# Weighting and summing the gathered tile of the first layer on GpSimd instead of VectorE

## The chip, the core and the metric

The kernel runs on one core of one Trainium2 chip. The metric is the device time of one execution in microseconds (us). One core has TensorE (PE in the profile, with its weight loads as PEld), VectorE (DVE), ScalarE (ACT), GpSimd (POOL) and SyncE (SP), which only starts DMA transfers here.

## What is computed

The whole kernel is a four-layer network on four images of 128 channels and 64 x 64 pixels, in fp32. The change is in the first layer alone, a deformable convolution. For each pixel and each of 8 groups of 16 channels, nine taps are read at places that the data itself moves:

```python
val = xf @ w_value + b_value
om = (xf @ w_off + b_off).reshape(N, P, G, OM)      # 18 offsets and 9 masks per group
...
for dy, dx, wgt in ((0, 0, (1 - ty) * (1 - tx)), (0, 1, (1 - ty) * tx), (1, 0, ty * (1 - tx)), (1, 1, ty * tx)):
    iy, ix = (y0i + dy, x0i + dx)
    acc = acc + gather(iy, ix) * (wgt * valid(iy, ix))[..., None]
out = (acc * mask[..., None]).sum(axis=3)
out = out.reshape(N, P, C) @ w_out + b_out
```

After it follow a batch norm and a SiLU. The layers behind it (a state-space convolution, attention maps with a feed-forward net, two mixtures of experts around an attention) are not touched.

## The kernel before

The first layer treats most pixels without a gather. For pixels whose offsets are all at most 1, the sum over the taps is a weighted sum over a 5 x 5 neighbourhood, and the neighbourhood is read as plain rows. The work goes in 32 **rounds**, 8 for each image; a round is a piece of 512 pixels (`r` is its number). In each round, for each of the five rows `k` of the neighbourhood:

- `multiply` is one VectorE instruction, `pr<-v,wt` of 128x2560, which multiplies the row's five shifted copies by their weights. `pr` has two buffers.
- `accumulate` is five TensorE matmuls `acc<-pr,ident` of 128x512, which add the five products up in PSUM.
- between them stand the steps of later rounds: `project` (TensorE, `psp<-wn,xr`), `evict` (VectorE, `omw<-psp,bn` and `vb<-psp,bn`), and on VectorE the interpolation weights of the next round (`tent`, `Q`, `t`, `wt`).

The pixels with an offset over 1 are rare. They are the **exceptions**: at most 128 of an image are collected by one-hot matmuls into one tile of 128 rows, and for this tile alone a 7 x 7 neighbourhood is gathered. The generator `exceptions(n)` does it for image `n`: 49 indirect DMAs that GpSimd issues, seven for each row `s` of the neighbourhood, each of which fetches one row of 128 channels per exception into `px`. `px` has two buffers, and row `s + 1` is issued before row `s` is used. Each row is multiplied by its weights (`total<-px,wt` for the first row, `px<-px,wt` for the other six) and added to `total` (six times `total<-total,px`). At the end seven matmuls `pe<-ident,total` sum the seven columns and turn the tile, and a second matmul applies `w_out`. The result, `tw`, is added to the rounds' outputs by the matmul `pO<-oT,tw` in `finish`. Last, `settle` adds the output `sl` to the image on GpSimd (`X<-X,sl`).

The order is written out by hand. `InOrder` keeps every instruction of an engine in program order, so an instruction that waits holds up all that stand behind it on its engine. The generator is advanced once for each `k` of a round:

```python
if r >= 0 and r % NQS == 1 and r < LAST_R:
    extra = exceptions(r // NQS)
...
if extra is not None:
    next(extra, None)
```

With `NQS = 8` it starts in an image's round 1. It yields twice for each row of the neighbourhood, so its last add stands at the end of the image's round 3, and the matmuls `pe<-ident,total` stand at the first step of round 4, in TensorE's order ahead of all further products of that round. Below, **idx** is the start of an image's first gather (it waits for the indices `idx` that VectorE makes), and **pe1** the start of `pe<-ident,total`. Nearly all instructions of the layer have line L81 in the profile, that of the helper in `InOrder`; so they are told apart by their tiles.

Of the kernel before, what the change touches and what calls it, by code (L numbers as in the profile page):

```python
# [11 lines left out]
ALU = mybir.AluOpType  # L12
# [75 lines left out]
class Kernel:  # L88
# [33 lines left out]
    def layer0(self):  # L122
# [7 lines left out]
        tc, nc, X = self.tc, self.nc, self.X  # L130
# [11 lines left out]
        with ExitStack() as outer:  # L142
            fp = outer.enter_context(tc.tile_pool(name="d0x", bufs=1))
            over = fp.tile([1, 1], I32, name="over")
            with ExitStack() as ctx:
# [142 lines left out]
                nc = InOrder(tc)  # L288
# [11 lines left out]
                def tents(om, m, r):  # L300

                    D = 2 * r + 1
                    o = om[:, 0:18 * m]
                    tent = wp.tile([P, D, 18 * m], F32, name=f"tent{r}", tag="tent")
                    ab = wp.tile([P, 18 * m], F32, name=f"ab{r}", tag="t0")
                    for d in range(-r, r + 1):
                        if abs(d) == r:
                            k = R2 + r - 1
                            nc.scalar.activation(tent[:, d + r, :], o, AF.Relu, bias=shift[:, k:k + 1],
                                                 scale=float(d // r))  # L310
                        else:
                            nc.scalar.activation(ab, o, AF.Abs, bias=shift[:, d + R2:d + R2 + 1])
                            nc.scalar.activation(tent[:, d + r, :], ab, AF.Relu, bias=self.ones[:, 0:1],
                                                 scale=-1.0)
                    return tent
# [135 lines left out]
                def exceptions(n):  # L451
                    oc = wp.tile([P, NO + 1, G], F32, name="oc")
                    ocf = oc.rearrange("p j g -> p (j g)")
                    nc.scalar.copy(ocf, rare[n][:, 0:(NO + 1) * G])
                    idx = wp.tile([P, W2, W2], I32, name="idx")
                    nc.vector.tensor_scalar(idx, reach, oc[:, NO, 0:1], None, ALU.add)
                    flat = tabs[n].rearrange("x y c -> (x y) c")
                    wt = wp.tile([P, W2, W2, G], F32, name="wt2")

                    def gather(s):  # L460
                        px = qp.tile([P, W2, P], F32, name="px")
                        for u in range(W2):
                            nc.gpsimd.indirect_dma_start(
                                out=px[:, u, :], out_offset=None, in_=flat,
                                in_offset=bass.IndirectOffsetOnAxis(ap=idx[:, s, u:u + 1], axis=0))
                            if u == 3:
                                yield
                        return px

                    px = yield from gather(0)  # L470
                    yield "weights"
                    for _ in weights(ocf, tents(ocf, G, R2), wt, G, R2):
                        pass
                    total = wp.tile([P, W2, P], F32, name="total")
                    for s in range(W2):
                        after = (yield from gather(s + 1)) if s + 1 < W2 else None
                        dst = px if s else total
                        nc.vector.tensor_tensor(
                            dst.rearrange("p u (g c) -> p (u g) c", c=CG),
                            px.rearrange("p u (g c) -> p (u g) c", c=CG),  # L480
                            wt[:, s].rearrange("p u g -> p (u g)").unsqueeze(2).to_broadcast([P, W2 * G, CG]),
                            ALU.mult)
                        if s:
                            nc.vector.tensor_tensor(total, total, px, ALU.add)
                        px = after
                        yield
                    ps = pt.tile([P, TG * P], F32, name="pe1", tag="pt")
                    for u in range(W2):
                        nc.tensor.matmul(ps[:, 0:P], total[:, u, :], self.ident, start=(u == 0), stop=(u == W2 - 1))
                    eT = sm.tile([P, P], F32, name="eT", bufs=1)  # L490
                    nc.scalar.copy(eT, ps[:, 0:P])
                    yield
                    ps = pt.tile([P, TG * P], F32, name="pe2", tag="pt")
                    nc.tensor.matmul(ps[:, 0:P], eT, w_out, start=True, stop=True)
                    tw = sm.tile([P, P], F32, name="tw", bufs=2)
                    nc.scalar.copy(tw, ps[:, 0:P])
                    mended[n] = tw
# [88 lines left out]
                for r in range(-4, LAST_R + 1):  # L586
# [5 lines left out]
                    if r >= 0 and r % NQS == 1 and r < LAST_R:  # L592
                        extra = exceptions(r // NQS)
# [79 lines left out]
                nc = plain  # L673
# [1815 lines left out]
```

## Time and profile before

| what | value |
| --- | --- |
| time, median of 3 runs | 5625.36 us (5615.98 to 5626.08) |
| profiled execution, its own time | 5626.52 us |
| its span (first to last instruction) | 5624.8 us |
| busy in the span: PE, DVE, ACT, POOL | 5034.6, 3967.9, 3095.8, 3025.3 us |
| idx to pe1, images 0 to 3 | 148.4 to 258.7, 410.2 to 521.6, 673.1 to 778.7, 927.6 to 1031.8 us |
| last `X<-X,sl` of the first layer | starts at 1141.82 us |

The first layer is thus about a fifth of the span. The profile shows one execution. Its 1.7 us beyond the span lie ahead of the first and behind the last instruction. A line of a group gives the number of instructions, their busy time, the mean of one in ns, and the idle time of the engine ahead of them with what ended it. A line of a table by stretch gives, for each engine, busy us and the number of instructions, then TensorE's granted clock (1.00 is full), the DMA share and GB/s.

### The profile page before, as it was taken

What the parts mean: (1) busy time and instruction counts of PE and PEld (TensorE: products, weight loads), DVE (VectorE), ACT (ScalarE), POOL (GpSimd) and SP (SyncE); (2) the same over time, 40 slices, a digit from 0 to 9 for tenths busy, and PEclk for the clock granted to TensorE, in tenths of its full rate; (3) what the DMA queues carried; (4) which work ended last, traced back from release to release, by engine and by line L of the source; (5) the groups of instructions that cost most, each with busy time, mean ns of one, the idle gap of its engine ahead of it and who ended that gap; (6) DMA issues with size and microseconds to landing.
All of it is one profiled execution on the core that took longest, in us unless ns stands there. A gap on an engine that the chain in (4) does not pass through costs nothing. (4 is left out here: it accounts for less than half of the span.)

```text
span 5624.8 us, 62917 instructions
## 1 busy us (share of the span) xinstructions
PE 5034.6 (90%) x21582; PEld 2263.2 (40%) x21582; DVE 3967.9 (71%) x7776; ACT 3095.8 (55%) x3721; POOL 3025.3 (54%) x2995
## 2 busy tenths in 40 slices
PE   6898988879999859999787999899989998999787
PEld 3454444436656523333443333333333333333343
DVE  6888988758876577886697655566566565665796
ACT  1122222146655445555421788878878887889431
POOL 0525344314444334544498666666666665667597
PEclk8999999989989779999898999999999999999899
DMA  5545454300000110000000000000000000000001
GB/s 173 129 128 127 130 129 121 94 6 3 14 16 16 43 40 1 1 1 1 6 31 30 1 1 1 1 1 1 1 1 1 1 1 1 1 1 1 5 1 60
DMA packets 66746, 185.23 MB, mean 33 GB/s; under 512 B 13158, under 2 KB 16038, under 8 KB 64744
## 3 DMA queue, kind: packets, MB, share of 16 engines
q1 hardware_dynamic: 55792, 163.68, 9.9%
q0 software_dynamic: 6272, 12.86, 1.4%
q10 hardware_dynamic: 4344, 4.50, 0.3%
q8 instruction: 174, 2.85, 0.2%
q14 instruction: 164, 1.34, 0.1%
HBM read 131.63 MB, written 49.36 MB: 32 GB/s over the span
## 5 line engine op out<-in xcount | busy, mean ns | idle before, releaser
L81 POOL TENSOR_TENSOR r<-r 128x512 f32<-128x512 f32 (+1 forms) x1088 | 1349.2, 1240 | 750.8 <-DVE r L81 688.3
L81 DVE TENSOR_TENSOR r<-r,num 128x1024 f32<-128x1024 f32 (+1 forms) x1088 | 964.6, 926 | 626.7 <-PE num L81 555.6
L81 PE MATMUL num<-F,N 32*128 32x512 f32 (+3 forms) x4608 | 1227.1, 614 | 70.2 <-DVE r L81 27.9
L81 PE MATMUL D<-F,G 32*128 32x512 f32 (+3 forms) x4608 | 1247.3, 607 | 33.6 <-ACT r L81 29.9
L81 ACT ACTIVATE r<-r 128x2048 f32<-128x2048 f32 (+4 forms) x610 | 1018.4, 1679 | 50.9 <-POOL r L81 3.8
L81 ACT ACTIVATE r<-D 128x1536 f32<-128x1536 f32 (+1 forms) x544 | 767.3, 1410 | 263.8 <-PE D L81 213.6
L81 PE MATMUL acc<-pr,ident 128*128 128x512 f32 x1600 | 748.3, 618 | 76.2 <-DVE pr L81 76.2
L81 PEld LDWEIGHTS D<-F,G 32*128 32x128 f32 x4608 | 415.6, 187 | 487.8 <-issue 344.9
L81 PE MATMUL acc<-r,v 128*128 128x512 f32 (+3 forms) x1152 | 608.0, 615 | 2.4 <-DVE aT L81 2.4
L1885 PE MATMUL pex<-w_expert_w,vT 128*128 128x512 f32 x1024 | 489.6, 617 | 79.5 <-DVE x L1888 79.4
L81 PEld LDWEIGHTS num<-F,N 32*128 32x128 f32 x4608 | 357.1, 186 | 468.5 <-SPq L81 340.1
L1895 POOL TENSOR_TENSOR x<-x 128x512 f32<-128x512 f32 (+2 forms) x576 | 472.5, 820 | 105.8 <-DVE x L1888 75.8
L81 PEld LDWEIGHTS acc<-pr,ident 128*128 128x128 f32 x1600 | 309.1, 198 | 435.9 <-issue 339.8
L81 DVE TENSOR_TENSOR pr<-v,wt 128x2560 f32<-128x2560 f32 x160 | 452.5, 2833 | 30.1 <-PE acc L81 24.3
L81 PE MATMUL pff<-hid,w_ffn_w2T 128*128 128x512 f32 x1024 | 468.2, 600 | 0.0
L81 POOL DMA_INDIRECT px<-tab,idx x196 | 331.8, 1693 | 227.8 <-DVE idx L81 159.2
L1888 DVE TENSOR_TENSOR x<-pex,gate 128x1024 f32<-128x1024 f32 x256 | 308.8, 1212 | 61.8 <-POOL X L1896 49.9
L81 POOL TENSOR_TENSOR X<-X,sl 128x512 f32<-128x512 f32 x32 | 87.7, 2740 | 491.8 <-ACT sl L81 491.8
L81 PEld LDWEIGHTS acc<-r,v 128*128 128x128 f32 x1152 | 177.1, 191 | 392.5 <-POOL r L81 217.3
L81 ACT ACTIVATE hid<-phh,cols 128x512 f32<-128x512 f32 x320 | 198.9, 685 | 223.9 <-PE phh L81 223.9
L1885 PEld LDWEIGHTS pex<-w_expert_w,vT 128*128 128x128 f32 x1024 | 183.2, 193 | 330.3 <-DVE x L1888 181.6
L81 POOL TENSOR_TENSOR Y<-y,tm 128x64 f32<-128x64 f32 x256 | 115.9, 473 | 323.4 <-DVE w L81 160.7
(562 smaller groups left out, 7139.3 us busy)
## 6 DMA issues: line engine op xcount, KB each, us to landing
v<-tab SPq DMA_DIRECT2D x320, 256.0 KB
oms<-omw SPq DMA_DIRECT2D x32, 432.0 KB
omr<-oms SPq DMA_DIRECT2D x32, 432.0 KB
X<-in_x_dram SPq DMA_DIRECT2D x8, 1024.0 KB
tab<-vb SPq DMA_DIRECT2D x64, 128.0 KB
o<-o SPq DMA_DIRECT2D x32, 256.0 KB
oin<-o SPq DMA_DIRECT2D x32, 256.0 KB
kept<-X SPq DMA_DIRECT2D x4, 2048.0 KB
```

The source lines that it names most:

```text
L81: return lambda *args, **kwargs: self.tc.keep_in_program_order(op(*args, **kwargs))
L1885: nc.tensor.matmul(pex[:, 4 * h:4 * h + 4, :], vT[:, k, :], ew[:, 512 * h:512 * (h + 1)], start=True, stop=True)
L1888: nc.vector.tensor_tensor(x, pex, gate[:, k, :].unsqueeze(2).to_broadcast([P, NE, P]), ALU.mult)
L1895: nc.gpsimd.tensor_tensor(x[:, 0:w, :], x[:, 0:w, :], x[:, w:2 * w, :], ALU.add)
```

## The change

The 13 elementwise instructions of each image's exceptions (seven multiplications by the weights and six additions, all 128x896 in fp32) move from VectorE's program to GpSimd's, at the same places in the program. GpSimd also issues the gathers that fill `px`; it now does so between these instructions. Nothing else in the source changes.

```diff
                     for s in range(W2):
                         after = (yield from gather(s + 1)) if s + 1 < W2 else None
                         dst = px if s else total
-                        nc.vector.tensor_tensor(
+                        nc.gpsimd.tensor_tensor(
                             dst.rearrange("p u (g c) -> p (u g) c", c=CG),
                             px.rearrange("p u (g c) -> p (u g) c", c=CG),
                             wt[:, s].rearrange("p u g -> p (u g)").unsqueeze(2).to_broadcast([P, W2 * G, CG]),
                             ALU.mult)
                         if s:
-                            nc.vector.tensor_tensor(total, total, px, ALU.add)
+                            nc.gpsimd.tensor_tensor(total, total, px, ALU.add)
                         px = after
                         yield
```

In the instruction streams of the changed kernel, GpSimd has for each image 14 gathers, one multiplication, then five times seven gathers, one multiplication and one addition, and last the multiplication and addition of the seventh row. VectorE's stream lacks the 52 instructions, and its other instructions keep their order. The first `pe<-ident,total` of each image waits for GpSimd where it waited for VectorE. On SyncE a few pairs of neighbouring stores (`tab<-vb`, `oms<-omw`) change places.

## Prediction

> **What bounds the kernel now.** I read the page first, then the busy time by stretch, with the cuts at each image's idx and pe1, then the tile px, then the timeline.
>
> The page's costliest groups give the work that shares an engine with the moved instructions:
>
> ```profile
> L81 POOL DMA_INDIRECT px<-tab,idx x196 | 331.8, 1693 | 227.8 <-DVE idx L81 159.2
> ```
>
> By stretch, idx to pe1 and pe1 to the next idx in turn:
>
> ```profile
> core 0: us, PE busy (x) PEld busy (x) DVE busy (x) ACT busy (x) POOL busy (x), PEclk, DMA share, GB/s
> 148.40:258.70 110.30, 88.64 (x226) 43.40 (x226) 99.79 (x147) 20.97 (x52) 81.03 (x49) 0.89 0.54 131
> 258.70:410.20 151.50, 151.26 (x455) 78.74 (x455) 132.33 (x215) 41.43 (x91) 25.38 (x8) 1.00 0.46 127
> 410.20:521.60 111.40, 87.93 (x226) 42.97 (x225) 99.34 (x147) 22.26 (x53) 81.64 (x49) 0.91 0.52 125
> 521.60:673.10 151.50, 151.26 (x455) 78.75 (x455) 132.77 (x216) 41.43 (x91) 25.26 (x8) 1.00 0.47 130
> 673.10:778.70 105.60, 87.72 (x222) 42.34 (x220) 88.28 (x127) 20.79 (x51) 84.75 (x49) 0.90 0.55 129
> 778.70:927.60 148.90, 147.74 (x438) 76.15 (x439) 134.82 (x204) 39.03 (x86) 20.79 (x8) 1.00 0.45 126
> 927.60:1031.80 104.20, 76.96 (x165) 32.72 (x163) 74.86 (x70) 18.56 (x43) 84.42 (x49) 0.87 0.52 114
> 1031.80:1150.00 118.20, 105.28 (x290) 49.45 (x290) 79.55 (x81) 25.30 (x53) 16.26 (x8) 0.97 0.25 67
> ```
>
> From pe1 to the next idx TensorE works without a break (151.26 of 151.50): it is the bound there, nothing lost earlier is made up. From idx to pe1 it idles a fifth of the time, and VectorE is the busiest (99.79 of 110.30 in image 0). But in images 2 and 3 VectorE idles too. The tile px says for what:
>
> ```profile
> L81 POOL DMA_INDIRECT px<-tab,idx x196: 940/1142/3560, 148.4 to 1025.7; - x196
> L81 DVE TENSOR_TENSOR px<-px,wt x24: 1073/1092/1125, 182.1 to 1029.6; 128x896 f32<-128x896 f32 x24
> L81 DVE TENSOR_TENSOR total<-total,px x24: 1091/1091/1093, 183.2 to 1030.7; 128x896 f32<-128x896 f32 x24
> ...
>   DMA px<-tab,idx: 40.5, 19
> ```
>
> GpSimd's gathers fill 95.9, 98.0, 99.4 and 99.0 us (first start to last end) of stretches of 110.3, 111.4, 105.6 and 104.2. So idx to pe1 has two chains of almost one length: VectorE's program, and GpSimd's 49 gathers. A gather takes 0.94 us at best and 1.69 in the mean. The timeline shows where the rest comes from:
>
> ```profile
> 148.07 2.82 DVE L81 TENSOR_TENSOR pr<-v,wt 128x2560 f32<-128x2560 f32 x1
> ...
> 148.45 3.48 POOL L81 DMA_INDIRECT px<-tab,idx  x1 [144.47 <-DVE idx L81]
> ...
> 281.28 2.82 DVE L81 TENSOR_TENSOR pr<-v,wt 128x2560 f32<-128x2560 f32 x1
> ...
> 281.56 3.67 POOL L81 TENSOR_TENSOR X<-X,sl 128x512 f32<-128x512 f32 x1 [5.69 <-ACT sl L81]
> ...
> 284.94 2.98 DVE L81 TENSOR_TENSOR pr<-v,wt 128x2560 f32<-128x2560 f32 x1 [0.83 <-PE acc L81]
> ```
>
> The gather that starts 0.4 us into a product ends 1.0 us after it; the addition that starts 0.3 us into one ends 1.15 us after it, and alone takes 1.26 (at 538.74). GpSimd waits for such a product's end.
>
> **What the Trainium skill says.** "SBUF — State Buffer", section Who interferes with whom: a VectorE instruction with two SBUF inputs contends with a GpSimd instruction that reads SBUF, and whoever came first holds the port pair for the whole instruction. The trace agrees, both ways: beside 3.67 against 1.26 above, one product at 803.00 that met an addition of 1.27 us took 3.93 instead of 2.82. Evictions, which read PSUM, delayed no gather (all of 21 that started in one took 0.94). The same section supposes that descriptor generation does not suffer from a tensor_tensor; here gathers that started in a product took 3.28 us in the median, and the measurement decides. "GPSIMD Engine Reference", section Elementwise — side-by-side cycle accounting, gives 4497 ns for an addition of 2048 columns, 2.2 ns for each. The trace gives 2.1, below.
>
> **The change part by part.** All is per image; the sum is at the end.
>
> *Off VectorE:* 13 x 1.09 = 14.2 us of work, and its waits for px (3.4, 5.0, 14.3 and 27.1 us in the four stretches, the short stops of px among them).
>
> *Onto GpSimd, the instructions themselves.* 896 columns stand in no row, so I take the two nearest families:
>
> ```profile
> L1895 POOL TENSOR_TENSOR x<-x 128x512 f32<-128x512 f32 x192 | 244.7, 1275 | 75.8 <-DVE x L1888 75.8
> ...
> L1895 POOL TENSOR_TENSOR x<-x 128x256 f32<-128x256 f32 x192 | 140.2, 730 | 15.0
> ...
> L81 POOL TENSOR_TENSOR ta<-tri,a 128x1024 f32<-128x1024 f32 x32 | 60.7, 1898 | 0.0
> ...
> L81 POOL TENSOR_TENSOR xw<-tm,wd 128x512 f32<-128x512 f32 x32 | 33.2, 1038 | 1.7 <-ACT tm L81 1.7
> ```
>
> Additions of two full operands: (1275 - 730)/256 = 2.13 ns a column, so 1275 + 384 x 2.13 = 2.09 us. Multiplications by a repeated weight: (1898 - 1038)/512 = 1.68, so 1.04 + 0.65 = 1.69 us. Together 7 x 1.69 + 6 x 2.09 = 24.4 us. From below all cost 1.69 (22.0); from above 2.4 each, with 0.3 us of idle as before every gather (31).
>
> *The gathers:* 49 x (0.94 + 0.30 idle) = 60.9 us without any port wait. Ahead of the last multiplication no further gather hides the landing any more: 2.9 us, as in image 3 today (1026.7 to 1029.6). GpSimd's chain without waits is thus 60.9 + 24.4 + 2.9 = **88.2 us**.
>
> *GpSimd's waits for the port.* Today's gathers average 98.1 us, so they wait 37.2; 2.7 of it behind the 13 instructions that leave VectorE. 34.5 stay. VectorE's other two-input instructions fill 58 to 64 us of a stretch; squares of their durations over twice the stretch give 0.6 us as the mean wait of an arrival at random, gathers have 0.7. I take 0.65 for each multiplication. An addition comes straight behind a multiplication that VectorE may have been waiting out, so VectorE then goes first: I take 1.1. That is 7 x 0.65 + 6 x 1.1 = 11.1 us. In sum 45.6 us of waits in 88.2 + 45.6 = 133.8 us, a share of **0.34**, as long as VectorE runs.
>
> *VectorE's new waits.* An instruction of GpSimd now holds the port for 1.7 to 2.1 us. VectorE wants it some 60% of the time; I take 1.0 us for each of 13, from 0 to 1.9. Its own program then takes, from idx, busy less 14.2, plus its waits for others (7.1, 7.1, 3.0, 2.2 us), plus 13: 105.7, 105.2, 90.1 and 75.9 us (77 in image 3, where TensorE needs as much).
>
> *The wait at pe1.* GpSimd's chain = 88.2 + 0.34 x the time that VectorE runs:
> image 0: 88.2 + 35.9 = 124.1, was 110.3: +13.8
> image 1: 88.2 + 35.8 = 124.0, was 111.4: +12.6
> image 2: 88.2 + 30.6 = 118.8, was 105.6: +13.2
> image 3: 88.2 + 26.2 = 114.4, was 104.2: +10.2
> The sum is **+50 us**. TensorE waits at pe1 some 18 to 37 us, and behind it stand all products of round 4; VectorE fills its two pr buffers and stops. TensorE then starts at half clock: after today's waits ten matmuls took 6.3 to 7.2 us instead of 4.46. I add 2 us an image, 8 in all, from 0 to 14.
>
> *At nothing:* the additions X<-X,sl stand behind pe1 in any case, ScalarE is busy 19% there, the stores that change places on SyncE come in pairs that few us separate, and the later layers move as a whole. The gathers' transfers are the same; they are spread out more.
>
> Against the profiled execution, 5626.5 + 58 = 5684.5; the median of the runs lies 1 us lower: **5684 us**.
>
> **Rivals.** Faster and slower mean by more than 0.2% (11 us), about what a measurement can tell from no change.
>
> *Faster: GpSimd had time to spare.* VectorE sheds 14 us and its waits for px, and would need 93, 92, 77 and 63 us if GpSimd held it up in nothing. For it speaks that VectorE is the busiest engine of the stretch. Against it, that GpSimd's gathers already fill nine tenths of it. The point is where GpSimd's chain falls below 108 us, so where its waits fall under 20 us an image, while the gathers alone wait 34 today. At half of that (17 us) the chain is 105: -3 an image; with none at all, 93, 92, 88 and 88, or -70. I take -35: 5591 us. 8%.
>
> *Slower still: the port alternates.* After each GpSimd instruction VectorE takes the port, and all 13 wait 2.2 us, close to a whole product; VectorE is held 1.9 us each. The share becomes (34.5 + 28.6)/151 = 0.42, VectorE runs 117, 117, 102 and 89 us, the chain is 137, 137, 131 and 126: +27, +26, +25, +22, and 10 for the clock: 5736 us. The back-to-back order of multiplication and addition speaks for it; against it, that many instructions of VectorE between products read PSUM or less than 1 us. 20%.
>
> *No change: made up behind pe1.* VectorE, ahead by two products, would have to speed up TensorE; at 151.26 of 151.50 it can't. 4%, about 5626 us.
>
> **How the numbers follow.** The waits as in the sum: 68%, 5684 us, with its own range 5642 (4 us an image, no clock) to 5735. Slower 0.88, within 0.2% 0.04, faster 0.08. The range 5640 to 5750 leaves out the faster cases, no change, and the far end of the alternation, under 20% together.
>
> **What would show it.** Right: in the table by stretch, idx to pe1 grows by 10 to 15 us while pe1 to the next idx stays at 149 to 151; TensorE waits for GpSimd's total at pe1, 15 us or more; GpSimd's 128x896 take 2 us at best and 2.3 to 3.2 in the mean; VectorE no longer waits for px, and some of its products take 3.5 us or more. Wrong: TensorE reaches pe1 after GpSimd is done, or the stretch shrinks; then the share of waits, 0.34, is the step that failed.

## The result and the profile after

The changed kernel takes 5700.03 us in the median of 6 runs (5683.76 to 5717.25), the kernel before, on the same chip, 5625.72 (5611.88 to 5641.41). The ratio is 1.0129, with a 95% interval of 1.0108 to 1.0149: 74 us slower. The profiled execution has a span of 5698.4 us, 73.6 more than that of before.

All of it is in the first layer. Its last `X<-X,sl` starts at 1213.60 us, where it started at 1141.82: 71.8 us later. What comes after it takes 4484.8 us in this profile, against 4483.0. Over all profiles of this study that rest moves between 4464 and 4492 us, although no kernel changed it. So the experiments below are judged by the start of the last `X<-X,sl`, beside the medians.

By stretch, with the cuts at idx and pe1 of each image as in the prediction:

```profile
core 0: us, PE busy (x) PEld busy (x) DVE busy (x) ACT busy (x) POOL busy (x), PEclk, DMA share, GB/s
147.50:267.40 119.90, 87.13 (x227) 43.09 (x225) 106.65 (x144) 21.14 (x53) 104.76 (x62) 0.88 0.52 124
267.40:421.30 153.90, 153.66 (x453) 80.50 (x454) 131.56 (x206) 41.27 (x90) 22.91 (x8) 0.98 0.45 122
421.30:548.20 126.90, 88.40 (x227) 43.58 (x225) 106.75 (x150) 22.42 (x54) 111.78 (x62) 0.85 0.48 120
548.20:701.70 153.50, 153.26 (x453) 80.38 (x454) 124.71 (x199) 41.27 (x90) 25.34 (x9) 0.99 0.43 120
701.70:826.70 125.00, 84.85 (x221) 41.25 (x219) 104.63 (x133) 20.95 (x52) 109.87 (x62) 0.86 0.50 121
826.70:976.70 150.00, 149.76 (x437) 77.92 (x438) 120.58 (x184) 38.76 (x85) 23.27 (x9) 0.98 0.42 115
976.70:1103.70 127.00, 69.43 (x165) 30.46 (x163) 82.05 (x73) 18.56 (x43) 111.92 (x62) 0.80 0.47 106
```

From idx to pe1 an image now takes 119.9, 126.9, 125.0 and 127.0 us, where it took 110.3, 111.4, 105.6 and 104.2: 67 us more in sum. From pe1 to the next idx it takes 1 to 2.5 us more, at a granted clock of 0.98 to 0.99 in place of 1.00, and TensorE is busy throughout. The tile px, and for its last line the tile total, say what happens in the first kind:

```profile
L81 POOL DMA_INDIRECT px<-tab,idx x196: 940/1034/3791, 147.5 to 1095.0; - x196
L81 POOL TENSOR_TENSOR px<-px,wt x24: 1705/1723/3675, 194.4 to 1099.8; 128x896 f32<-128x896 f32 x24
L81 POOL TENSOR_TENSOR total<-total,px x24: 2067/2084/4677, 196.2 to 1101.6; 128x896 f32<-128x896 f32 x24
L81 POOL TENSOR_TENSOR total<-px,wt x4: 1721/1724/1726, 176.2 to 1006.9; 128x896 f32<-128x896 f32 x4
...
  PE pe L81: 99.0, 4
```

A multiplication takes 1.72 us and an addition 2.08 on GpSimd, and TensorE waits 99 us at pe1, in four waits. In the kernel before this last line was

```profile
  PE pe L81: 2.2, 1
```

GpSimd's instructions do not wait for their gathers to land: in the tile px, the list of what engines sat idle for has `DMA px<-tab,idx` at 40.5 us in the kernel before and not at all in this one. The longest wait at pe1 is in image 3, in the timeline of TensorE:

```profile
1043.47 13.14 PE L81 MATMUL acc<-pr,ident 128*128 128x512 f32 x30 [1.22 <-DVE pr L81]
1103.71 3.36 PE L81 MATMUL pe<-ident,total 128*128 128x128 f32 x14 [47.10 <-POOL total L81]
1106.86 3.47 PE L81 MATMUL acc<-pr,ident 128*128 128x512 f32 x6
```

So TensorE, less its wait, gets to pe1 110.5, 110.1, 99.2 and 79.9 us after idx, 31.7 us earlier in sum than pe1 stood before, and then waits 9.4, 16.8, 25.8 and 47.1 us. VectorE has lost 14.2 us of work an image and its waits for px, and images 0 and 1 get nothing from it. The timeline shows what takes it back, first a product, then additions of one column in the tile `fl`:

```profile
447.69 4.65 DVE L81 TENSOR_TENSOR pr<-v,wt 128x2560 f32<-128x2560 f32 x1 [1.85 <-PE acc L81]
...
447.93 1.73 POOL L81 TENSOR_TENSOR total<-px,wt 128x896 f32<-128x896 f32 x1
...
196.36 2.36 DVE L81 TENSOR_TENSOR fl<-fl 128x1 f32<-128x1 f32 x3
...
196.18 2.08 POOL L81 TENSOR_TENSOR total<-total,px 128x896 f32<-128x896 f32 x1
```

In the kernel before, three such additions were

```profile
170.14 0.55 DVE L81 TENSOR_TENSOR fl<-fl 128x1 f32<-128x1 f32 x3
```

The product takes 4.65 us instead of 2.82, and three tiny additions 2.36 us instead of 0.55, while GpSimd's instruction runs. Taking each VectorE instruction of a stretch over the usual duration of its kind, VectorE is held up 19.0, 13.6, 18.1 and 8.1 us from idx to pe1.

### The profile page after: what moved, and what is told of

It is laid out like the page before. It is cut to its first block, busy times and chain, and to the rows that moved or that the text cites. A ratio compares the mean times of both kernels' runs of the same rounds, so it can differ in the third digit from the quotient of the medians.

```text
span 5698.4 us, 62841 instructions
## 1 busy us (share of the span) xinstructions
PE 5037.1 (88%) x21582; PEld 2270.4 (40%) x21582; DVE 3970.2 (70%) x7724; ACT 3095.5 (54%) x3721; POOL 3129.8 (55%) x3047
## 5 line engine op out<-in xcount | busy, mean ns | idle before, releaser
L81 ACT ACTIVATE r<-r 128x2048 f32<-128x2048 f32 (+4 forms) x610 | 1018.4, 1679 | 50.9 <-POOL r L81 3.9
```

Source lines behind the costliest of these rows:

```text
L81: return lambda *args, **kwargs: self.tc.keep_in_program_order(op(*args, **kwargs))
```

## The experiments

The theory: gathers and sums stand one behind the other on GpSimd, this **chain** is now longer than everything else from idx to pe1, and TensorE waits for its end. The rival: the loss is **VectorE being held at the port** by GpSimd's new instructions.

All numbers below, in one table. "Last X" is the start of the last `X<-X,sl`, less the 1141.8 us of the kernel before; the ratio is to the runs of the kernel before on the same chip. The waits at pe1 and the stretches are sums over the four images.

| kernel | median us | ratio, 95% interval | last X, us | wait at pe1, us | idx to pe1, us |
| --- | --- | --- | --- | --- | --- |
| before | 5625.7 | 1 | 0 | 2.2 | 431.4 |
| changed | 5700.0 | 1.0129 (1.0108 to 1.0149) | +71.8 | 99.0 | 498.7 |
| short_gathers | 5616.5 | 0.9980 (0.9971 to 0.9988) | -6.9 | 0 | 428.3 |
| shed_sums | 5572.8 | 0.9902 (0.9882 to 0.9922) | -50.9 | 0 | 362.2 |
| late_pe1 | 5653.7 | 1.0049 (1.0031 to 1.0068) | +26.7 | 48.1 | a round more |
| six_more_sums | 5746.1 | 1.0206 (1.0183 to 1.0228) | +122.9 | 130.3 | 549.9 |
| three_rows | 5653.6 | 1.0039 (1.0022 to 1.0055) | +25.0 | 2.3 | 456.4 |
| before_late_pe1 | 5641.9 | 1.0012 (1.0003 to 1.0021) | +8.7 | 0 | a round more |
| spread_vector | 5605.5 | 0.9953 (0.9936 to 0.9970) | -26.7 | 4.1 | a round more |

The first four after the changed kernel ran beside runs of the kernel before with a median of 5628.4 us, the last three beside 5633.2.

**short_gathers** cuts the chain and keeps the new instructions.

```diff
-                        for u in range(W2):
+                        nc.gpsimd.memset(px[:, 2:, :], 0.0)
+                        for u in range(2):
...
-                            if u == 3:
+                            if u == 1:
```

> Five of the seven gathers of each row are left out, and GpSimd clears their five columns of px instead (0.6 us), so the sums miss most of the neighbourhood; all 13 products and sums of an image stay on GpSimd as in the changed kernel. Theory of the chain (TensorE waits at pe1 because gathers and sums stand one behind the other on GpSimd): GpSimd's chain falls from 120 to 127 us to about 60, the waits at pe1 (9.4, 16.8, 25.8 and 47.1 us in the changed kernel) are gone, and pe1 comes when VectorE and TensorE get there, about 110, 110, 99 and 80 us after idx: 5590 to 5605 us. Rival (the loss is VectorE being held at the port by the 13 instructions): these are all still there, so 5680 us or more.

TensorE no longer waits at pe1, and the loss is gone: the chain is what made the changed kernel slower. It ends 76 to 78 us after idx here, where 60 were expected, and still 18 us or more ahead of pe1. But the time is only 12 us under that of before, where 23 to 38 were expected. The table by stretch, images 0 to 3:

```profile
148.10:263.90 115.80, 90.57 (x226) 43.86 (x225) 101.47 (x134) 20.98 (x52) 66.06 (x33) 0.88 0.42 109
415.60:530.50 114.90, 90.30 (x226) 43.91 (x225) 102.13 (x134) 22.25 (x53) 66.32 (x33) 0.87 0.42 108
682.20:784.40 102.20, 86.41 (x220) 41.59 (x219) 98.68 (x117) 20.80 (x51) 68.60 (x33) 0.92 0.45 115
931.90:1027.30 95.40, 76.33 (x165) 32.90 (x164) 85.00 (x59) 18.55 (x43) 69.36 (x33) 0.89 0.41 101
```

VectorE is busy 101.5 us in image 0, 1.7 us more than before, with 13 instructions fewer: it is held up 16.4, 17.1, 20.5 and 19.9 us, more than the 14.2 that it shed. So the holds that the rival names are there, though they are not the cause of the loss: they take back what VectorE was relieved of.

**shed_sums** takes the work off VectorE without putting it on GpSimd.

```diff
-                        nc.vector.tensor_tensor(
-                            dst.rearrange("p u (g c) -> p (u g) c", c=CG),
+                        if s == 0:
+                            nc.vector.tensor_tensor(
+                                dst.rearrange("p u (g c) -> p (u g) c", c=CG),
...
-                        if s:
-                            nc.vector.tensor_tensor(total, total, px, ALU.add)
```

> Only the product of the first row stays, on VectorE; the other 12 products and sums of an image are left out on both engines, and all gathers are still issued. It prices what VectorE can gain by shedding them, with nothing put on GpSimd. Theory of the chain: VectorE loses 13.1 us of work and its waits for px (3.4, 5.0, 14.3, 27.1 us), so idx to pe1 takes about 94, 93, 89 and 76 us instead of 110, 111, 106 and 104: near 5546 us (5535 to 5570). Rival (VectorE's load in this stretch does not matter, TensorE is the bound there): above 5600 us. The difference to the run with few gathers is what the port holds cost: about 50 us if VectorE, held 8 to 19 us an image in the changed kernel, gets nothing out of the move.

VectorE's load in this stretch is worth a lot: idx to pe1 falls to 102.5, 101.1, 83.9 and 74.7 us, the time by 55.5. Nothing holds VectorE up here (under 1 us an image). The gain is some 25 us less than expected. One part is that VectorE waits more for TensorE: `rstd` and `bn`, two steps of the batch norm, wait 7.6 us in image 0, where they waited 3.2. And in image 3 the gathers go on for 38 us behind pe1, with the `X<-X,sl` behind them on GpSimd; ScalarE cannot reuse sl:

```profile
ACT sl L81 <- issue: 24.4, 1, 24.4
```

The first of these additions starts at 1003.80 us, right behind the last gather, and TensorE idles 10.3 us in turn; from pe1 to the last X image 3 takes 125.2 us in place of 110.0. Between this run and short_gathers lie 66 us in idx to pe1 and 44 us in the medians. That is mostly the price of the holds, 74 us in sum in short_gathers; the two runs also differ in the engine of the first product and in the gathers.

**late_pe1** leaves everything in place and lets a round of 29 us pass before TensorE asks for the sum; the image's first pieces are finished a round later too.

```diff
+                    for _ in range(5):
+                        yield
                     ps = pt.tile([P, TG * P], F32, name="pe1", tag="pt")
...
-                    aT = qp.tile([P, TG * P], F32, name="aT", bufs=4)
+                    aT = qp.tile([P, TG * P], F32, name="aT", bufs=5)
...
-                    for k, qs in ((4, (0, 1)), (5, (2, 3)), (6, (4,)), (7, (5,)), (8, (6, 7))):
+                    for k, qs in ((5, (0, 1)), (6, (2, 3)), (7, (4, 5)), (8, (6, 7))):
```

> The changed kernel with pe1 and the finishing of the image's first pieces put one round later (five more yields ahead of pe1, one more buffer for aT). All work is done. Theory of the chain: a round of some 29 us now lies over GpSimd's chain. It covers the waits of images 0 to 2 (9.4, 16.8, 25.8 us) all but a few us and 27 of the 47 us of image 3, so about 75 to 80 us come back: 5615 to 5640 us, level with the kernel before. Rival (VectorE held at the port): the holds stay as they are and so does the loss, 5680 us or more.

45 us come back by the last X and 46 in the medians. The rival, which had 5680 us or more, is thus excluded, but 75 to 80 were expected. The waits at pe1 are 0, 0, 14.7 and 33.4 us; the estimate had about 0, 0, a few and 20. Its table by stretch shows the reason, images 2 and 3:

```profile
681.10:817.10 136.00, 108.60 (x295) 53.61 (x293) 128.01 (x169) 26.82 (x66) 120.89 (x62) 0.93 0.58 139
941.30:1080.10 138.80, 92.56 (x220) 40.61 (x218) 104.33 (x88) 23.63 (x54) 123.69 (x62) 0.87 0.50 116
```

GpSimd's chain itself has become longer, 136.0 and 138.8 us instead of 125.0 and 127.0. Its gathers wait 47.2 and 43.6 us beyond their 0.94 us each, where they waited 34.0 and 36.2. In the changed kernel VectorE stands still while TensorE waits at pe1, and issues 15 products from idx to pe1 in each image; here it goes on, and issues 20 in images 2 and 3. The wait at pe1 partly pays for itself.

**before_late_pe1** is the control: the same edit on the kernel before.

> The control for the late pe1: the kernel before, all 13 instructions on VectorE, with pe1 and the finishing of the first pieces one round later. All work is done. Theory of the chain: TensorE does not wait at pe1 in this kernel (2.2 us in image 3 alone), so putting it later brings nothing: 5618 to 5632 us. Rival (a later finishing is worth something by itself, or costs something): off by more than 10 us, and then the 46 us that the late pe1 gave to the changed kernel are not all the wait at pe1.

It costs 8.7 us by the last X, and by the medians too, where no change was expected. So it is no gain by itself, and the changed kernel with a late pe1 stands 18.0 us behind a kernel before with the same late pe1. Where the 8.7 us arise was not followed; the instructions that wait for px wait 48.1 us in place of 45.1, which is part of it at most.

**six_more_sums** doubles the six additions.

```diff
                             nc.gpsimd.tensor_tensor(total, total, px, ALU.add)
+                            nc.gpsimd.tensor_tensor(px, total, px, ALU.add)
```

> The changed kernel with each of the six sums of an image done twice on GpSimd (the second result is thrown away). Theory of the chain: pe1 waits for GpSimd in all four images already, so each further 2.07 us shows up whole: 6 x 2.07 = 12.4 us an image and up to 3 us of further port waits, 50 to 62 us in all: 5750 to 5762 us. Rival (only the holds of VectorE count): 24 more instructions that hold it 1.0 us each where it still runs, 10 to 24 us: 5710 to 5725 us.

Idx to pe1 grows by 51.2 us and the last X by 51.1 us, 12.8 us for each 12.5 us of GpSimd's work; the medians differ by 46. That is a slope of one, as the chain has it, and two to five times what the rival had (10 to 24 us). VectorE is held longer as well (30.1 and 24.6 us in images 0 and 1), but TensorE's wait for GpSimd is still the end of every stretch.

**three_rows** puts 9.3 us of the 24.5 on GpSimd.

```diff
-                        nc.gpsimd.tensor_tensor(
+                        eng = nc.gpsimd if s < 3 else nc.vector
+                        eng.tensor_tensor(
...
-                            nc.gpsimd.tensor_tensor(total, total, px, ALU.add)
+                            eng.tensor_tensor(total, total, px, ALU.add)
```

> The changed kernel with only the first three rows' products and sums on GpSimd (five instructions, 9.3 us an image) and the other eight on VectorE. All work is done. Theory of the chain: the gathers' 98 us grow by 9.3 us, then come the last landing and VectorE's last product and sum (5 us), so pe1 stands some 112 us after idx in every image, where it was 110, 111, 106 and 104: 15 to 25 us slower than before, 5640 to 5655 us. Rival (a few instructions still fit into GpSimd's idle time): within 8 us of before.

As the chain has it. There is no room on GpSimd even for five instructions: 25.0 us, 6.2 an image, of the 9.3. Since the last sum is VectorE's again, it is VectorE that waits, as the tile px shows:

```profile
  DMA px<-tab,idx: 68.4, 10
...
  DVE px L81: 68.1, 9
```

In the kernel before, the second of these lines was

```profile
  DVE px L81: 45.1, 15
```

The growth of 23.0 us is nearly all of the 25.0; what the port took from VectorE (22 us over the four images) is as much as the 21.8 of work that it shed. With 0, 9.3, 24.5 and 37.0 us of arithmetic an image on GpSimd, the last X stands at 0, 25, 72 and 123 us: a slope of 0.7 to 0.8 at first, and of one at the end.

**spread_vector** follows from this: leave the sums on VectorE, and space them as GpSimd's gathers come. It has late_pe1's edits of aT and of the order of finishing, without the five yields, on the kernel before, and:

```diff
                         px = after
                         yield
+                        if s < 5:
+                            yield
```

> A version that may beat both: the 13 instructions on VectorE as before, but the rows of the neighbourhood are three steps apart in place of two (one more yield behind each of the first five rows), so that they lie over four rounds, and pe1 one round later. All work is done. Theory: VectorE no longer reaches a product before its gather has landed (its waits for px were 3.4, 5.0, 14.3 and 27.1 us), some 6.6 us of its work an image move into round 4, where TensorE is the bound, and GpSimd holds it up nowhere: 35 to 60 us less than before, 5570 to 5595 us. Rival (only taking the 12 instructions off VectorE altogether helps, as in the run without them): less than 15 us gained, above 5610 us.

It beats both kernels: 0.9953 of the kernel before (0.9936 to 0.9970), 27.7 us less in the medians, and its last X is 98.5 us ahead of the changed kernel's. That lies between the theory (35 to 60 us) and its rival (less than 15). The waits for px do shrink, from 45.1 us to

```profile
  DVE px L81: 11.5, 4
```

but images 0 and 1 gain little. VectorE waited for px only some 6 us there in the control with a late pe1 (15 and 26 us in images 2 and 3), and its own work fills nine tenths of their stretches (122.5 of 136.0 us in image 0). Their idx to pe1, over four rounds, takes 136.0 and 134.4 us, against 139.6 and 138.5 in the control; images 2 and 3 take 118.8 and 117.3, against 136.0 and 130.5.

## Why the prediction was right, and its terms

5684 us was forecast, with 5640 to 5750, and 5700 measured. The likeliest case is the one that happened, and short_gathers, six_more_sums and three_rows tie it to GpSimd's chain. Step by step:

- *The instructions on GpSimd:* 1.69 and 2.09 us against 1.72 and 2.08. Both prices came from rows of the same kind and other widths, and held to 2%.
- *The gathers without waits:* 60.9 us, measured 60.7. *The last landing*, 2.9 us, was a mistake of reading: the two instructions of the sixth row stand between the last gather and the last multiplication and cover it. GpSimd's chain without waits is 85.2 us, not 88.2.
- *GpSimd's waits:* the mis-sized term. The chains of 119.8, 126.9, 125.0 and 127.0 us leave 34.6, 41.7, 39.8 and 41.8 us for waits, 158 in sum; the share of 0.34 of VectorE's running time gave 128.5. The gathers alone wait 31.4, 38.4, 34.0 and 36.2 us, nearly as much as before. The error is the share. GpSimd waits for instructions of VectorE, for the products above all, and of these 15 start in every stretch, in image 3 too, where VectorE is done after 91 us. (In late_pe1 it is 20 in images 2 and 3, and the gathers wait 47.2 and 43.6 us.) Counted per instruction instead of per time, the waits of before, less the 2.7 us behind the moved instructions, would have given 34 us an image for the gathers; 35 came. The 13 new instructions wait 3 to 6 us an image in place of the 11 assumed, most of them not at all; one or two an image wait 1.9 to 2.6 us, so that the longest addition takes 4.68 us.
- *VectorE's new waits:* 13 us an image taken, 14.7 measured in the mean. The forecast had VectorE ready at 105.7, 105.2, 90.1 and 77 us, TensorE got to pe1 at 110.5, 110.1, 99.2 and 79.9.
- *The wait at pe1:* 18 to 37 us forecast, 9 to 47 measured. The growth of idx to pe1 was forecast as 50 us and was 67; it is largest in image 3 (22.8), where the forecast had its least (10.2), for the reason above.
- *The clock:* 8 us taken for slow starts behind pe1; the stretches behind it grew by 2.4, 2.0, 1.1 and -0.1, in sum 5.4.
- *The sum:* 58 us forecast, 73.6 in the profile. The chain without waits was taken 12 us too long over the four images, the waits 29 us too short. That 5684 lies only 16 us from 5700 is thus in part luck: two errors partly cancel.
- *The signs:* idx to pe1 grew by 9.6 to 22.8 us (10 to 15 forecast), pe1 to the next idx took 150 to 154 us (149 to 151), and TensorE waited 9.4 us in image 0 (15 or more). GpSimd's 128x896 were quicker than the signs had it: 1.7 us at best and 2.19 in the mean, not 2 and 2.3 to 3.2. VectorE waited for px no more, and some products took over 4.6 us. One reading was off without consequence: VectorE's other two-input instructions filled 63 to 68 us of a stretch before, not 58 to 64.
- *The rivals:* "GpSimd had time to spare" fell, with three_rows; of the relief that it had for VectorE (idx to pe1 in 93, 92, 77 and 63 us) shed_sums shows the larger part (102.5, 101.1, 83.9 and 74.7), but GpSimd's holds take it away. "The port alternates", at 5736, is not what happens: 10 to 12 of the 13 run at full speed, and it is VectorE that waits. "Made up behind pe1" fell: nothing is made up there.

## What to carry to other kernels

Before work is moved to an engine that is "only" 54% busy, look at the stretch: what it already does there, and by when its last result is needed. Here GpSimd's gathers filled nine tenths of the stretch, so each us put behind them came out as 0.7 to 1 us ahead of the matmul that takes the sum. And the moved arithmetic counted twice here: once on the receiver, GpSimd, and once more on the giver, VectorE, in waits for the port as long as what it was relieved of (14.7 us an image against 14.2).

## What the runs showed of the hardware that was not expected

A VectorE instruction of a single column (`fl<-fl`, 0.16 us) waits for a GpSimd instruction as long as a product does: it is held for up to 2 us, and so is the comparison with a column of scalars, `ohc<-count,slot`, with one wide input (1.30 us in place of 0.28 beside a 1.29 us addition in the kernel before). And a GpSimd multiplication that started 0.24 us into a product ran at its full speed, 1.73 us, while the product took 1.83 us more: starting first did not secure the port in that case, nor in two more of the same kind (products of 4.67 and 4.90 us).
